# Second block's first steps: combine quarters ahead of the next transposes, and the feed-forward at a distance of seven steps

## The chip, the cores and the metric

One NeuronCore of one Trainium2 chip runs the whole program. The metric is the device time of one execution in microseconds. Every array is float32. The engines are TensorE (PE, with its weight loads PEld), VectorE (DVE), ScalarE (ACT), GpSimd (POOL) and SyncE (SP, which issues most of the DMAs).

## What is computed

The reference has two blocks over 2 sequences of 1024 tokens with 256 features. The lines that matter here, cut:

```python
# block 0: attention with a field, then a soft mixture of 64 experts
combine = softmax(logits.reshape(b, m, n * p))        # per token over 2048 slots
x = x + einsum('bnpd,bmnp->bmd', y, combine)           # "combine"
# block 1: a rotation of x, then two layers of this
x1 = rotated(x)                                        # one 256x256 matrix per token
for l in range(2):
    q, k, v = split(shift(x1) @ wqkv[l])
    q, k = rotary(l2norm(q) * qs), rotary(l2norm(k) * ks)
    x1 = x1 + local_attention(q, k, v) @ wo[l]         # windows of 128, each with the one before
    h = layernorm(shift(x1)) * lg + lb                 # over 256 features
    a, g = split(h @ w1[l] + b1[l])                    # 682 wide each
    x1 = x1 + (a * gelu(g)) @ w2[l] + b2[l]
x = x + x1
```

## The kernel before, in words

The change lies in the last part of the kernel, a loop over steps `s` whose order is written out by hand: PE, DVE, ACT and POOL execute their instructions in the order in which the loop emits them (`manual_schedule` names the four engines). SP's DMAs are not in that list; each is issued when its data and its buffer are ready.

**Attention.** There are 32 windows of 128 tokens: two layers, two sequences, eight windows. In step `s`, window `s+2` is projected (`project`, `rotate_parts`, `values`, `norms`, `rotated`), window `s+1` is transposed (`turn`), window `s` gets its scores for two groups of four heads (`scores`, `maxima`, `weights`, `divide`), and windows `s-1` and `s-2` are finished (`turn_e` transposes the weights, `mix` multiplies with the values). After each fourth window `project_out` writes 512 tokens of `xb`.

**Feed-forward.** A chunk is 512 tokens, eight chunks in all. `forward(s - LAG)` runs one quarter of a chunk at the end of a step: `gate` 0 to 5 (the gated first matrix in six pieces, the last a short one of 42 rows), `feed` (the second matrix) and, for the next chunk, `centre` (mean by a matmul with `ones_d`, subtraction on DVE, square on ACT) and `normalise` (variance by a matmul, square root on ACT, reciprocal and product on DVE, scale and shift on POOL).

**Combine.** Block 0's combine is not finished when the loop begins. Its products for sequence 1 run beside the first attention steps, at the points "a", "c" and "b" of a step, as a list `mixing` of pairs `(q, jj)`: quarter `q` of 256 tokens, and four of 16 expert groups `jj`. `turn_w(q, jj)` makes eight transposes of softmax rows into one two-bank PSUM tile, copies it to `xb` (DVE for odd `jj`, ACT for even), and fetches logits of later rows. `combine(q, jj)` multiplies by the experts' outputs (16 PE instructions of 256 columns). `weigh(i)` and `scale(i)` are the softmax of row block `i`: a maximum on DVE, an Exp on ACT, a reciprocal and product on DVE. `READY` says at which points they stand. `rotate(h)` makes 512 tokens of block 1's input.

`PARTS` puts quarters at the points: three in steps -2 and -1, two (at "a" and "b") in steps 0 to 4, so that at "a" of steps 0 to 4 the tile that is turned has odd `jj` and goes through DVE, and at "b" an even one through ACT.

**PSUM.** `two_banks` hands out two tiles (`ps_b`). While `mixing` is not empty, the third two-bank tile (`ps_c`) holds the combine's sum; afterwards the three go round in turn (`ring`). `project`, `scores`, `turn_w`, `turn_e`, `turn`, `rotate`, `project_out`, `gate` and `feed` all take their tile from here.

The order at point "a" of a step, before:

```python
project(s + 2); rotate_parts(s + 2); mix(s - 2, 1); scores(s, 0)
beside(s, "a")            # turn_w of the next quarter, then combine of this one
turn_e(s - 1, 0)
maxima(s, 0); weights(s, 0); values(s + 2)
```

Of the kernel before, what the change touches and what calls it, by code (L numbers as in the profile page):

```python
# [91 lines left out]
def tile_kernel(ctx: ExitStack, tc: tile.TileContext, a: dict, out: bass.AP):  # L92
# [80 lines left out]
    def wide(name):  # L173
        return ps_s.tile([P, 2, 512], F32, tag="s", name=name)

    def pair(name):
        return ps_t.tile([P, 2, 512], F32, tag="t", name=name)
# [147 lines left out]
    def mix(s):  # L325

        u, n, j0 = s // 16, s % 16 // 8, s % 8
        b, g = units[u]
        po = pair("po")[:, 0, :]
        for j in (j0, j0 + 1):  # L330
            for hh in range(4):
                at = (4 * g + hh) * VW
                nc.tensor.matmul(  # L333
                    po[32 * hh : 32 * hh + 32, :],
                    v[b][:, j, at : at + 32],
                    es[s + j - j0, hh // 2][:, hh % 2, :],
                    start=(j == j0),
                    stop=(j > j0),
                )
        for x in range(4):  # L340
            es.pop((s + x // 2, x % 2))
        if j0 == 0:
            obs[u, n] = at2.tile([P, 512], F32, tag="ob", name=f"ob{u}_{n}")
            nc.scalar.copy(obs[u, n], po)
            return
        if s >= STEPS - LEAD:
            nc.vector.tensor_tensor(obs[u, n], obs[u, n], po, ALU.add)
            return
        part = at2.tile([P, 512], F32, tag="part", name="part", bufs=1)
        nc.scalar.copy(part, po)  # L350
        nc.gpsimd.tensor_tensor(obs[u, n], obs[u, n], part, ALU.add)  # L351
# [466 lines left out]
    def row(i):  # L818
        return ebig[:, i % 4, :]
# [19 lines left out]
    def turn_w(q, jj):  # L839

        pt = wide("pe")
        for j in range(4):
            for i in range(2):
                nc.tensor.transpose(
                    pt[:, j // 2, (j % 2 * 2 + i) * P : (j % 2 * 2 + i + 1) * P],
                    row(2 * q + i)[:, (4 * jj + j) * P : (4 * jj + j + 1) * P],
                    ident,
                )
        wTs[q, jj] = xb[:, jj % 2, 1, 1 : 1 + S].rearrange("p (x n) -> p x n", x=2)
        if jj % 2:  # L850
            nc.vector.tensor_copy(wTs[q, jj], pt)
        else:
            nc.scalar.copy(wTs[q, jj], pt)  # L853
        for i in (2 * q + 4, 2 * q + 5):
            if i < T // P:
                fetch(i, jj)
# [156 lines left out]
    with tc.manual_schedule(  # L1013
# [15 lines left out]
        mixing, ring = [None], []  # L1029
# [164 lines left out]
        def divide(i, hg):  # L1194
            e, lo, den = scs.pop((i, hg))
            nc.vector.reciprocal(den, den)  # L1196
            engine = nc.vector if hg else nc.gpsimd
            for c in range(2):
                for x in range(2):
                    engine.tensor_scalar(e[:, x, c, lo:], e[:, x, c, lo:], den[:, x, c : c + 1], None, ALU.mult)  # L1200
            es[i, hg] = e
# [54 lines left out]
        def chunk(f):  # L1256

            return f // (B * 2), f // 2 % B, f % 2 * 512
# [27 lines left out]
        def gate(f, n):  # L1286

            l = chunk(f)[0]
            if n == 0:
                us[f] = fa["u"]  # L1290
            pt = two_banks("pga")
            gl = fa["gl"][:, n % 2, :]
            if n < NW1:
                for x, lo in ((0, W1G + n * P), (1, W1A + n * P)):
                    for k in range(2):
                        nc.tensor.matmul(  # L1296
                            pt[:, x, :], load["w1"][:, k, lo : lo + P], hcs[f][:, k, :], start=(k == 0), stop=(k == 1)
                        )
                pg, pa, m, g0 = pt[:, 0, :], pt[:, 1, :], P, 0
            else:  # L1300
                for k in range(2):
                    nc.tensor.matmul(
                        pt[: TG + TAIL, 0, :], load["w1"][:, k, W1T:W1N], hcs[f][:, k, :], start=(k == 0), stop=(k == 1)
                    )
                pg, pa, m, g0 = pt[TG : TG + TAIL, 0, :], pt[:TAIL, 0, :], TAIL, TG
            nc.scalar.activation(gl[:m, :], pg, AF.Gelu, bias=col(f"b1g{l}", n)[g0 : g0 + m, :])  # L1306
            nc.vector.scalar_tensor_tensor(
                us[f][:m, n, :], pa, col(f"b1a{l}", n)[:m, :], gl[:m, :], ALU.add, ALU.mult
            )
# [29 lines left out]
        def forward(at):  # L1339

            f, k = divmod(at, 4)
            if at == -2:
                centre(0)
            if at == -1:
                normalise(0)
            if not 0 <= f < CHUNKS:
                return
            if k == 0:
                gate(f, 0)
                gate(f, 1)  # L1350
            if k == 1:
                gate(f, 2)
                gate(f, 3)
                if f + 1 < CHUNKS:
                    centre(f + 1)
            if k == 2:
                gate(f, 4)
                gate(f, 5)
                if f + 1 < CHUNKS:
                    normalise(f + 1)  # L1360
            if k == 3:
                feed(f)


# [2 lines left out]
        mixing = [(q, jj) for q in range(4, 8) for jj in range(4)]  # L1367
# [12 lines left out]

        def beside(s, point):
            if point in PARTS.get(s, ""):
                if len(mixing) > 1:
                    turn_w(*mixing[1])
                q, jj = mixing[0]
                combine(q, jj)
                mixing.pop(0)
                if (q, jj) in ((4, 1), (6, 1)):
                    rotate(q // 2 - 1)
            for f, i in READY.get((s, point), ()):  # L1390
                f(i)

        LAG = 8
        fa = {}
        for s in range(-2, LAG + 4 * CHUNKS):
            now, before, nxt, new = (0 <= s + d < WINDOWS for d in (0, -1, 1, 2))

            if new:
                project(s + 2)
                rotate_parts(s + 2)  # L1400
            if 0 <= s - 2 < WINDOWS:
                mix(s - 2, 1)
            if now:
                scores(s, 0)
            beside(s, "a")
            if before:
                turn_e(s - 1, 0)
            if now:
                maxima(s, 0)
                weights(s, 0)  # L1410
            if new:
                values(s + 2)
                keep_values(s + 2)
            beside(s, "c")
            if now:
                scores(s, 1)
                maxima(s, 1)
            if before:
                mix(s - 1, 0)
            if nxt:  # L1420
                turn(s + 1)
            if now:
                weights(s, 1)
            if new:
                norms(s + 2)
            beside(s, "b")
            if 0 <= s - 2 < WINDOWS and (s - 2) % 4 == 3:
                project_out((s - 2) // 4)
            if before:
                turn_e(s - 1, 1)  # L1430
            if now:
                divide(s, 0)
            if new:
                rotated(s + 2)
            forward(s - LAG)
            if now:
                divide(s, 1)
            if s == 5:

                rotate(3)  # L1440
                f = xp.tile([P, 4 * NS], F32, tag="e", name="f")
                at = 0
                for name, k, n in (("u", NF, 512), ("w2", NF, D), ("yo", 2, 512), ("rs", 1, 512), ("sq", 2, 512), ("gl", 2, 512)):
                    fa[name] = f[:, at : at + k * n].rearrange("p (k n) -> p k n", k=k)
                    at += k * n
                fa["rs"] = fa["rs"][:, 0, :]
                fa["hc"] = xin.tile([P, 2, 2, 512], F32, tag="x1", name="hc")
                load["w2"] = fa["w2"]
                load["w1"] = xp.tile([P, NE // 4 * D], F32, tag="y1", name="w1")[:, : 2 * W1N].rearrange(
                    "p (k n) -> p k n", k=2  # L1450
                )
                weights2(0, "w1", "w2")
            if s + 2 == B * NWIN - 1:
                weights2(1, "wqkv", "tabs")
            if s == B * NWIN + 2:
                weights2(1, "wo")
            if s == LAG + 4 * (CHUNKS // 2) - 2:
                weights2(1, "w1")
            if s == LAG + 4 * (CHUNKS // 2) - 1:
                weights2(1, "w2")  # L1460
# [118 lines left out]
```

## Time and profile before

| | before |
|---|---|
| median of 3 runs (lowest to highest) | 1710.03 us (1709.95 to 1711.98) |
| the profiled execution | 1710.05 us |
| its span, first to last instruction | 1708.3 us |
| PE busy | 1659.0 us (97%) |
| DVE, ACT, POOL busy | 950.6 (56%), 830.1 (49%), 426.2 (25%) |
| step -2 starts (first `project`) | 889.89 us |
| step 5 starts | 1044.91 us |
| first `gate` | 1112.52 us |
| end of the last attention step's PE work (`project_out`) | about 1647 us |

The profiled execution lies 1.75 us above its span and 0.02 us above the median, so its rows can be set against the median without a correction. Two things help in reading what follows. A PE row's duration is partly modelled, and matmuls overlap, so the time that PE spends on a piece of work is read from one start to the next (16 combine matmuls: 3.46 us from the first start to the next piece's start). And a wait in brackets at the end of a row is the engine's idle time just before it, with the instruction that ended it.

### The profile page before, as it was taken

Reading aid. Unit: us, or ns where it says so; the run is one execution under the profiler, and the core shown is the slowest. Engines: PE = TensorE matmul, PEld = TensorE weight load, DVE = VectorE, ACT = ScalarE, POOL = GpSimd, SP = SyncE. Lnnn points to the kernel's source line nnn. Section 1 sums busy time; section 2 is a strip of 40 time slices with the busy share of each in tenths; the row PEclk is TensorE's granted clock in tenths of the full one; section 3 lists DMA queues with packets and bytes.
Section 4 is the critical chain, followed back from the end, with each engine's and each line's share of the span. In section 5 each row is a group of like instructions: output and inputs, shape, how many; then the busy total and the mean of one; then the engine's idle time right before and its main releaser. Section 6 shows DMA issues by size and latency. Waiting matters only on the chain.

```text
span 1708.3 us, 22359 instructions
## 1 busy us (share of the span) xinstructions
PE 1659.0 (97%) x8684; PEld 842.9 (49%) x8684; DVE 950.6 (56%) x1622; ACT 830.1 (49%) x1329; POOL 426.2 (25%) x716
## 2 busy tenths in 40 slices
PE   8999999999999999999999899999999999999998
PEld 4333443443433444444787566555555555555543
DVE  5767767766773322243445666756565656574522
ACT  1456556656667322243233444655555656565520
POOL 3101101111110100000102334645554544354301
PEclk9999999999999999999999999999999999999999
DMA  5100000000000534555542002000100001000001
GB/s 150 50 13 13 1 13 14 1 14 12 1 1 1 170 116 159 160 172 165 189 129 71 21 1 75 1 0 1 62 1 13 1 1 34 17 1 25 1 25 37
DMA packets 49593, 82.55 MB, mean 48 GB/s; under 512 B 4508, under 2 KB 24816, under 8 KB 49232
## 3 DMA queue, kind: packets, MB, share of 16 engines
q1 hardware_dynamic: 46944, 75.29, 14.5%
q0 software_dynamic: 1584, 5.29, 1.0%
q8 instruction: 68, 1.11, 0.3%
q10 hardware_dynamic: 960, 0.56, 0.1%
q14 instruction: 37, 0.30, 0.1%
HBM read 55.95 MB, written 20.97 MB: 45 GB/s over the span
## 4 chain that ended last, share of the span: by engine, by line
PE 86%; DVE 7%; ACT 4%; POOL 1%; issue 1%; DMA 1%; DVEq 0%; ACTq 0%; POOLq 0%
PE sc L314 9%; PE pga L1296 8%; PE po L333 7%; PE lg L754 7%; PE sl L780 6%; PE pm L282 6%; PE cmb L865 6%; PE py L1319 5%; PE pq L1061 4%; PE pwo L1250 3%; PE sc L1150 3%; PE pe L1211 3%; PE po L1230 3%; PE pv L1117 2%; ACT e L322 2%; PE pqk L252 2%
## 5 line engine op out<-in xcount | busy, mean ns | idle before, releaser
L289 DVE TENSOR_REDUCE mx<-pm 128x2 f32<-128x1024 f32 x256 | 304.5, 1220 | 87.5 <-PE pm L282 83.5
L322 ACT ACTIVATE e<-sc 128x1024 f32<-128x1024 f32 x256 | 253.8, 1023 | 91.4 <-PE pm L282 53.3
L282 PE MATMUL pm<-km,qm 32*128 32x512 f32 x1024 | 271.1, 635 | 3.3 <-DVE mx L289 2.1
L314 PE MATMUL sc<-qs,km 32*128 32x512 f32 x1024 | 254.4, 614 | 9.0 <-ACT e L322 8.1
L351 POOL TENSOR_TENSOR ob<-ob,part 128x512 f32<-128x512 f32 x43 | 54.5, 1267 | 421.4 <-ACT part L350 421.4
L314 PEld LDWEIGHTS sc<-qs,km 32*128 32x128 f32 x1024 | 85.7, 184 | 133.9 <-ACT e L322 68.0
L1200 POOL TENSOR_SCALAR e<-e,den 128x256 f32<-128x256 f32 (+1 forms) x128 | 131.0, 1036 | 58.1 <-DVE den L1196 58.1
L1296 PE MATMUL pga<-hc,w 128*128 128x512 f32 x320 | 141.1, 593 | 0.0
L1167 DVE CUSTOM_DVE_ANT_0 e<-sc,mask,zn 128x256 f32<-128x256 f32 (+1 forms) x256 | 103.5, 462 | 45.4 <-PE sc L1150 45.4
L1184 ACT ACTIVATE e<-e,nmx 128x256 f32<-128x256 f32 (+1 forms) x256 | 123.5, 486 | 3.1 <-DVE nmx L1167 2.9
L333 PE MATMUL po<-e,v 128*32 128x512 f32 x1024 | 123.8, 600 | 0.7 <-ACT e L322 0.6
L1085 POOL TENSOR_TENSOR t<-raw,tabs 128x512 f32<-128x512 f32 x64 | 80.2, 1274 | 168.2 <-ACT raw L1075 165.9
L780 PE MATMUL sl<-dsp,xb 128*128 128x512 f32 x256 | 116.7, 600 | 2.0 <-ACT dsp L769 2.0
L865 PE MATMUL cmb<-xb,y 128*128 128x256 f32 x512 | 117.6, 383 | 0.2 <-ACT xb L853 0.2
L1061 PE MATMUL pq<-wqo,xa 128*128 128x512 f32 x256 | 115.7, 595 | 0.7 <-ACT xa L892 0.7
L754 PE MATMUL lg<-phi,xa 128*128 128x512 f32 x256 | 115.9, 595 | 0.3 <-ACT xa L407 0.3
L865 PEld LDWEIGHTS cmb<-xb,y 128*128 128x128 f32 x512 | 95.8, 192 | 12.8 <-ACT xb L853 0.5
L1075 ACT COPY raw<-pq 128x1024 f32<-128x1024 f32 x32 | 32.4, 1012 | 134.7 <-PE pq L1061 134.7
L764 DVE TENSOR_TENSOR l<-lg,keep 128x512 f32<-128x512 f32 x32 | 22.1, 691 | 135.8 <-ACT keep L762 135.8
L1306 ACT ACTIVATE f<-pga,cols 128x512 f32<-128x512 f32 (+1 forms) x48 | 32.9, 686 | 125.8 <-PE pga L1296 118.4
L1296 PEld LDWEIGHTS pga<-hc,w 128*128 128x128 f32 x320 | 59.2, 190 | 67.7 <-issue 66.3
L282 PEld LDWEIGHTS pm<-km,qm 32*128 32x128 f32 x1024 | 77.2, 183 | 28.7 <-DVE mx L289 14.8
(199 smaller groups left out, 2429.2 us busy)
## 6 DMA issues: line engine op xcount, KB each, us to landing
lgd<-keep SPq DMA_DIRECT2D x64, 256.0 KB, 2.4
w<-in_ffn_W SPq DMA_DIRECT2D x16, 1024.0 KB, 7.3
ebig<-lgd SPq DMA_DIRECT2D x64, 256.0 KB, 3.3
wqo<-in_wqkv SPq DMA_DIRECT2D x2, 1536.0 KB, 8.9
w<-in_w SPq DMA_DIRECT2D x2, 1386.0 KB, 6.1
km<-hk SPq DMA_DIRECT2D x32, 64.0 KB, 2.3
qm<-hq SPq DMA_DIRECT2D x32, 64.0 KB, 2.4
phi<-in_phi SPq DMA_DIRECT2D x1, 2048.0 KB, 7.5
```

The lines of the kernel that those rows point to most:

```text
L282: nc.tensor.matmul(pm[:, x, :], qm[u % 2][r, i * P : (i + 1) * P], km[u % 3][r, n * 512 : (n + 1) * 512], start=True, stop=True,)
L289: nc.vector.tensor_reduce(mxs[hu][:, i % 4, 2 * half : 2 * half + 2, n], pm, AX.X, ALU.max)
L314: nc.tensor.matmul(sc[:, x, :], km[u % 3][r, j * P : (j + 1) * P], qs[u % 2][r, n * 512 : (n + 1) * 512], start=True, stop=True,)
L322: nc.scalar.activation(e, sc, AF.Exp, scale=1.0 / HD0**0.5)
L333: nc.tensor.matmul(po[32 * hh : 32 * hh + 32, :], v[b][:, j, at : at + 32], es[s + j - j0, hh // 2][:, hh % 2, :], start=(j == j0), stop=( ...
L754: nc.tensor.matmul(lg[:, b, :], xa[:, k, b, 1 + m * P : 1 + (m + 1) * P], phi[:, k, n * 512 : (n + 1) * 512], start=(k == 0), stop=(k == 1),)
L780: nc.tensor.matmul(accs[n][b][:, c, :], xo_tm[:, b * 8 + m, c * P : (c + 1) * P], d[:, b, :], start=(m == 0), stop=(m == 7),)
L865: nc.tensor.matmul(acs[q][:, c, :], y[b][:, 4 * jj + j, c * P : (c + 1) * P], eT[:, j // 2, j % 2 * 256 : (j % 2 + 1) * 256], start=(jj == ...
L1061: nc.tensor.matmul(pq[:, x, :], shifted(xa, k, b, w * WIN, P), load["wqkv"][:, k, x * 512 : (x + 1) * 512], start=(k == 0), stop=(k == 1),)
L1184: nc.scalar.activation(e[:, x, c, lo:], e[:, x, c, lo:], AF.Exp, bias=nmx[:, x, c : c + 1], scale=-1.0, accum_out=den[:, x, c : c + 1],)
L1200: engine.tensor_scalar(e[:, x, c, lo:], e[:, x, c, lo:], den[:, x, c : c + 1], None, ALU.mult)
L1296: nc.tensor.matmul(pt[:, x, :], load["w1"][:, k, lo : lo + P], hcs[f][:, k, :], start=(k == 0), stop=(k == 1))
```

## The change

Three things. In `beside`, the quarter's `combine` now comes first and the next quarter's `turn_w` after it. `LAG` goes from 8 to 7, so that each quarter of a feed-forward chunk runs one step earlier; with it the set-up of the feed-forward's buffers and its weight loads moves ahead of `forward` in step 5, and `rotate(3)` from the end of step 5 to before its scores. In `forward`, `centre` of the next chunk moves from after gates 2 and 3 to between gates 4 and 5, and `normalise` from after gate 5 to the front of the next quarter, ahead of `feed`. Since `LAG` shrinks by one and these move one quarter on, both keep their step relative to the attention. The diff, whole but for blank lines:

```diff
             if k == 1:
                 gate(f, 2)
                 gate(f, 3)
+            if k == 2:
+                gate(f, 4)
                 if f + 1 < CHUNKS:
                     centre(f + 1)
-            if k == 2:
-                gate(f, 4)
                 gate(f, 5)
+            if k == 3:
                 if f + 1 < CHUNKS:
                     normalise(f + 1)
-            if k == 3:
                 feed(f)
...
             if point in PARTS.get(s, ""):
-                if len(mixing) > 1:
-                    turn_w(*mixing[1])
-                q, jj = mixing[0]
+                q, jj = mixing.pop(0)
                 combine(q, jj)
-                mixing.pop(0)
+                if mixing:
+                    turn_w(*mixing[0])
                 if (q, jj) in ((4, 1), (6, 1)):
                     rotate(q // 2 - 1)
...
-        LAG = 8
+        LAG = 7
...
                 mix(s - 2, 1)
+            if s == 5:
+                rotate(3)
             if now:
                 scores(s, 0)
...
                 rotated(s + 2)
-            forward(s - LAG)
-            if now:
-                divide(s, 1)
             if s == 5:
-                rotate(3)
                 f = xp.tile([P, 4 * NS], F32, tag="e", name="f")
...
                 weights2(0, "w1", "w2")
+            forward(s - LAG)
+            if now:
+                divide(s, 1)
```

## The prediction

> **What bounds the kernel now.** First the engines' busy times, then PE's waits in the two stretches that the change touches, then the timeline of single steps.
>
> ```profile
> PE 1659.0 (97%) x8684; PEld 842.9 (49%) x8684; DVE 950.6 (56%) x1622; ACT 830.1 (49%) x1329; POOL 426.2 (25%) x716
> ```
>
> PE is the bound, and the change removes no PE work. It can only win or lose idle PE time. The waits (line waited for: us in total, times, longest), first for 880 to 1120 us, then for 1120 us to the end:
>
> ```profile
> PE pe L844 <- DVE t L1083: 5.7, 5, 1.8
> PE pe L844 <- DVE nmx L1167: 2.8, 2, 2.6
> PE pe L1211 <- POOL e L1200: 2.5, 5, 0.6
> ```
>
> ```profile
> PE sc L1150 <- DVE t L1083: 2.3, 4, 0.6
> PE pe L1211 <- DVE e L1200: 1.8, 3, 1.3
> ```
>
> L844 is `turn_w`: its PSUM tile is the one that `project` used, and it waits for DVE (L1083) to empty it, in steps 0 to 4. Step 3 in the timeline:
>
> ```profile
> 1005.54 1.13 PE L1150 MATMUL sc<-qkT 64*128 64x256 f32 x8
> ...
> 1006.30 1.21 DVE L1083 TENSOR_TENSOR t<-pq,tabs 128x1024 f32<-128x1024 f32 x1
> ...
> 1007.56 1.09 PE L844 MATMUL pe<-ident,ebig 128*128 128x128 f32 x8 [0.88 <-DVE t L1083]
> 1008.49 3.63 PE L865 MATMUL cmb<-xb,y 128*128 128x256 f32 x16
> 1008.69 1.22 DVE L851 COPY xb<-pe 128x1024 f32<-128x1024 f32 x1 [1.19 <-PE pe L844]
> 1009.83 0.47 DVE L1167 CUSTOM_DVE_ANT_0 e<-sc,mask,zn 128x256 f32<-128x256 f32 x1
> ...
> 1011.95 1.04 PE L1211 MATMUL pe<-ident,e 128*128 128x128 f32 x8
> ```
>
> See two things: the 0.88 us wait, and that today the product (3.46 us) covers the copy (L851) which frees the tile for `turn_e` (L1211). Two PSUM tiles are in play and `scores` holds the other until `maxima` (L1167), which DVE runs after the copy.
>
> [...] clock 0.93 in 930.5 to 953.5, and a combine that takes 5.0 us instead of 3.46 just after an idle 2.56 us. [...] Moving `normalise` away from the gates adds one load per chunk, on an ACT that is 49% busy: taken as free under `feed` (10.9 us of PE).
>
> **Part A: product first.** Durations from the rows: product 3.46, eight transposes 0.87, DVE copy 0.2 + 1.22 + 0.05 = 1.45 after the last transpose.
>
> *Point "a", steps 1 to 4.* The product now covers the wait for L1083. But `turn_e` follows the transposes at once and waits 1.45 for the copy. Gaps that go (issue to issue): 1.42, 0.84, 0.96, 0.96. So 0, +0.6, +0.5, +0.5.
>
> *Point "b".* `turn_w`'s ACT copy is then followed only by `turn_e` (0.87), and `project` needs its tile: 0.2 + 1.0 + 0.05 - 0.87 = +0.4 in steps 2 and 3. In step 1 `rotate` covers it, and the wait of 0.4 for `maxima` goes: -0.4. In step 2 a like wait of 0.3 goes.
>
> *Step 2's DVE chain.* Behind the copy stand `scale`, `weigh` and `maxima`, and PE waits for the last:
>
> ```profile
> 985.41 1.22 DVE L851 COPY xb<-pe 128x1024 f32<-128x1024 f32 x1 [1.19 <-PE pe L844]
> ...
> 986.74 1.29 DVE L837 TENSOR_SCALAR ebig<-ebig,den 128x2048 f32<-128x2048 f32 x1
> 987.94 2.28 DVE L828 TENSOR_REDUCE nmx<-ebig 128x1 f32<-128x2048 f32 x1
> ...
> 990.33 0.48 DVE L1167 CUSTOM_DVE_ANT_0 e<-sc,mask,zn 128x256 f32<-128x256 f32 x1
> ...
> 992.08 1.13 PE L1150 MATMUL sc<-qkT 64*128 64x256 f32 x8 [0.65 <-DVE nmx L1167]
> ```
>
> Scores end at 983.44; product and transposes put the copy at 987.98 instead of 985.41: the chain and this L1150 come 2.57 later. With -0.3 and +0.4 at "b" step 2 is +2.6 (its 0.6 at "a" lies inside). PE then idles 2.8 us in one piece[...]: +1.3.
>
> *Steps -1 and 0.* Product (5,1) has only `turn` (0.87) between its copy and itself: +0.6. Step 0 took 22.99 us (930.49 to 953.48) with 15.99 of work. Now its copy ends at 941.0, scale at 942.4, `weigh`'s maximum at 944.75, `maxima` at 945.9; `turn(1)`, ready at 941.9, waits for that. Then product, transposes, and `project(3)` at 951.1, plus 1.15 for the half clock up to 948.2: 952.3, so steps -1 and 0 together -1.2.
>
> Sum of A: -1.2 - 0.4 + 2.6 + 1.3 + 0.9 (step 3) + 0.5 (step 4) = **+3.7**. The logits' fetches on SP come 3.46 later; the last of rows 12 and 13 lands near 915, and its reader on DVE starts at 928. If that margin of 13 were gone, it would be paid in full.
>
> **Part B: LAG 7.** *Step 5*: `rotate` ahead of the scores covers `turn_e`'s POOL divide (row 1.37 instead of 0.87): -0.5. `centre(0)` directly follows `project_out` and must wait for its DVE add (0.2 + 1.22 + 0.05, less `turn_e` 0.87): +0.6. The w1 load was issued at 1043.17 and lands in about 6 us; its first user moves from 1112 to about 1097, so it stays hidden.
>
> *Steps 7 and 8.* Step 8 starts at 1097.30 and needs 7.7 of PE work to its second scores, but:
>
> ```profile
> 1101.26 3.35 DVE L1279 RECIPROCAL f<-f 128x512 f32<-128x512 f32 x1
> ...
> 1109.05 0.71 PE L1150 MATMUL sc<-qkT 64*128 64x128 f32 x8
> ```
>
> 3.95 is lost: POOL's divide has no feed-forward to hide under, `normalise`'s reciprocal holds DVE, and a slow window follows. With gates in step 7, step 8 loses nothing. `normalise(0)` moves to step 6: from its matmul to the second scores it took 13.45 (1095.58 to 1109.05), which puts step 7's at 1093.45 instead of 1091.69: +1.75. Net -2.2.
>
> *Steady steps.* The four waits of L1150 for L1083 (2.3) follow `normalise` at a step's end. With `feed`'s 10.9 behind it they go: -2.3. `centre` between gates 4 and 5 has the same add ahead of it and 3.43 of gate 4 as cover (6.87 before): free, and at worst 0.5 each for 7 chunks if DVE is late. At the layer's turn POOL multiplies the new tables up to 1238.0, and the step gets 1.7 shorter: up to 0.5 there.
>
> *Tail.* Step 31:
>
> ```profile
> 1610.19 0.30 PE L1211 MATMUL pe<-ident,e 128*128 128x128 f32 x1 [1.27 <-DVE e L1200]
> ...
> 1613.21 12.85 PE L1319 MATMUL py<-f 128*128 128x512 f32 x24 [0.84 <-DVE nmx L1167]
> ```
>
> 1.8 for the divide behind the reciprocal, 0.84, and `feed` 1.9 over its 10.9 at half clock: 4.5. After, `feed` covers the reciprocal in step 30 and gates stand in 31: about 0.5 is left. New: in step 34 `normalise(7)` has only gate 5 (1.72) over subtractions and square (0.2 + 1.28 + 0.1 + 1.06): +0.9. Net -3.1. One `feed` quarter fewer at the end changes no work.
>
> Sum of B: +0.1 - 2.2 - 2.3 - 3.1 = **-7.5**. Late next is `turn_e` at "a", for its own tile.
>
> **Sum**: +3.7 - 7.5 = -3.8; 1710.05 - 3.8 = **1706.2**, the same against the median, which is 0.02 lower. About 0.2% (3.4 us) is what a measurement of this kernel can tell from no change; the forecast sits just past that.
>
> **The cases.** (1) As worked out, 50%: 1702.5 to 1709, by slow windows more or fewer[...] and 0.5 per small cover. (2) Product first pays in full, 15%: `turn_e` gets the free tile and DVE its copy in time. Then 5.7 + 2.8 of waits and the slow window's 1.5 go: 1710.05 - 10 - 7.5 = 1692.5; with half of the DVE chain left, about 1700. For it speaks that PE waits most at L844, against it DVE's order in the rows above. (3) Slower, 10%: the new idle pieces at "a" of steps 1 to 4 and in steps 7 and 34 each halve the clock.[...] Against it: `turn_e`'s and `turn_w`'s transposes lie on both sides[...]. (4) The waits move rather than go, 25%: DVE's reciprocal and `feed`'s adds delay other tiles and B brings 3 instead of 7.5: 1710.7. Against it: `feed`'s 10.9 exceeds the reciprocal's 3.35, product 1.23 and POOL's 1.75 together.
>
> Faster by over 0.2%: 33 of case 1, all 15 of (2), 5 of (4) = 53%. Within: 17 and 18 = 35%. Slower: 10 and 2 = 12%. The range 1699 to 1712.5 leaves out half of (2) and the slower end.
>
> **What would show it.** Right: L844 without waits for L1083; instead L1211 waiting about 1.4 for L851 in four steps, and a second scores in step 2 waiting near 2.8 for L1167; no wait of L1150 for L1083 in the steady steps; no wait of L1211 for L1200 before the last feeds. Wrong: `turn_e` at "a" without a wait, or waits of L1211 for DVE that come back after each `feed`.

## The result, and the profile after

The changed kernel takes 1709.62 us (median of 14 runs, 1707.89 to 1710.87), the kernel before 1709.82 us on the same chips (14 runs). The ratio is 0.9996, with a 95% interval of 0.9988 to 1.0004. That is no change which can be told from none: between 2.1 us faster and 0.7 us slower. The forecast was 1706.2 us.

The two halves of the change are both large, and they cancel. The page of the profiled execution (1709.74 us, span 1707.9) has the same PE work:

```profile
PE 1658.3 (97%) x8684; PEld 844.7 (49%) x8684; DVE 949.1 (56%) x1622; ACT 839.7 (49%) x1335; POOL 425.8 (25%) x716
```

PE's waits after, for 880 to 1120 us and then to the end (line waited for: us in total, times, longest):

```profile
PE pe L1211 <- DVE xb L851: 4.2, 3, 1.4
PE pt L1135 <- DVE nmx L1167: 3.8, 1, 3.8
PE sc L1150 <- DVE nmx L1167: 2.5, 1, 2.5
PE sc L1150 <- DVE t L1083: 1.8, 1, 1.8
PE pe L1211 <- DVE den L836: 1.4, 1, 1.4
PE pe L1211 <- POOL e L1200: 1.1, 2, 0.6
...
```

```profile
PE po L1230 <- ACT eT L1217: 1.5, 2, 1.2
PE pvar L1276 <- ACT f L1269: 0.7, 1, 0.7
PE pwo L1250 <- ACT oT L1241: 0.7, 1, 0.7
```

All waits of L844 (8.5 us) are gone, and so are the four of L1150 for L1083 in the steady steps and those for L1200 near the end. In their place stand waits of `turn_e` (L1211) for the copy L851, and two long ones for `maxima` (L1167). The row with `den L836` is the same wait for the copy; another short DVE instruction ended last.

Step 3 in the timeline, the same place as before:

```profile
1011.34 1.14 PE L1150 MATMUL sc<-qkT 64*128 64x256 f32 x8
...
1011.61 1.20 DVE L1083 TENSOR_TENSOR t<-pq,tabs 128x1024 f32<-128x1024 f32 x1
1012.41 3.73 PE L865 MATMUL cmb<-xb,y 128*128 128x256 f32 x16
...
1015.97 1.04 PE L844 MATMUL pe<-ident,ebig 128*128 128x128 f32 x8
1017.05 1.22 DVE L851 COPY xb<-pe 128x1024 f32<-128x1024 f32 x1 [4.24 <-PE pe L844]
1018.19 0.47 DVE L1167 CUSTOM_DVE_ANT_0 e<-sc,mask,zn 128x256 f32<-128x256 f32 x1
1018.42 1.06 PE L1211 MATMUL pe<-ident,e 128*128 128x128 f32 x8 [1.41 <-DVE xb L851]
```

L1083 ends at 1012.8, long before the transposes, so the old wait is gone. DVE then idles 4.24 us until the transposes give it the copy, and PE stands for the length of that copy.

In step 2 the late copy moves a whole chain on DVE, and PE waits for its end:

```profile
989.71 1.22 DVE L851 COPY xb<-pe 128x1024 f32<-128x1024 f32 x1 [3.86 <-PE pe L844]
...
992.24 2.28 DVE L828 TENSOR_REDUCE nmx<-ebig 128x1 f32<-128x2048 f32 x1
...
994.62 0.47 DVE L1167 CUSTOM_DVE_ANT_0 e<-sc,mask,zn 128x256 f32<-128x256 f32 x1
...
996.37 1.21 PE L1150 MATMUL sc<-qkT 64*128 64x256 f32 x8 [2.51 <-DVE nmx L1167]
```

In step 0 it is the same chain with `turn` at its end:

```profile
941.16 1.22 DVE L851 COPY xb<-pe 128x1024 f32<-128x1024 f32 x1 [2.86 <-PE pe L844]
...
943.69 2.28 DVE L828 TENSOR_REDUCE nmx<-ebig 128x1 f32<-128x2048 f32 x1
...
946.08 0.34 DVE L1167 CUSTOM_DVE_ANT_0 e<-sc,mask,zn 128x128 f32<-128x128 f32 x1
...
947.29 1.97 PE L1135 MATMUL pt<-ident,t 128*128 128x128 f32 x8 [3.81 <-DVE nmx L1167]
...
949.05 5.54 PE L865 MATMUL cmb<-xb,y 128*128 128x256 f32 x16
```

Before, the longest wait in this step was 2.56 us, and one product was slow:

```profile
947.41 1.27 PE L844 MATMUL pe<-ident,ebig 128*128 128x128 f32 x8 [2.56 <-DVE nmx L1167]
948.48 5.17 PE L865 MATMUL cmb<-xb,y 128*128 128x256 f32 x16
```

After, both pieces of work behind the wait are slow: the transposes take 1.76 us to the next start instead of 0.93, the product 5.38 instead of 3.46. The table of stretches (start and end in us, length, busy time of PE, PEld, DVE, ACT, POOL, then PE's clock, the DMA share and GB/s) gives the clock for steps 0 and 2, where 1.00 is full speed:

```profile
932.34:955.30 22.96, 19.15 (x87) 13.87 (x85) 13.28 (x32) 11.63 (x25) 5.94 (x16) 0.85 0.16 47
...
979.78:1006.69 26.91, 22.56 (x125) 16.29 (x125) 17.14 (x39) 13.92 (x27) 9.63 (x18) 0.94 0.00 1
```

In step 0 the clock is 0.50 from 946.10 to 952.93, in step 2 from 997.30 to 1000.71. Before, it is 0.50 from 948.19 to 951.60 in step 0, from 1105.20 to 1108.61 in step 8 and from 1613.78 to 1617.19 in the `feed` of step 31. The forecast and the expectations call a stretch like these a slow window or a half-clock window.

Near the end the reciprocal now lies inside `feed`:

```profile
1606.99 11.05 PE L1319 MATMUL py<-f 128*128 128x512 f32 x24
1610.69 3.35 DVE L1279 RECIPROCAL f<-f 128x512 f32<-128x512 f32 x1 [3.90 <-ACT f L1278]
1614.08 1.22 DVE L1280 TENSOR_TENSOR hc<-hc,f 128x1024 f32<-128x1024 f32 x1
```

Lengths of the steps, from one `project` to the next, in the two profiled executions (us):

| | before | after | difference | forecast |
|---|---|---|---|---|
| step -1 | 19.02 | 19.72 | +0.70 | +0.6 |
| step 0 | 22.99 | 22.96 | -0.03 | -1.8 |
| step 1 | 24.68 | 24.48 | -0.20 | -0.4 |
| step 2 | 22.83 | 26.91 | +4.08 | +3.9 |
| step 3 | 21.87 | 23.05 | +1.18 | +0.9 |
| step 4 | 22.05 | 22.85 | +0.80 | +0.5 |
| steps -1 to 4 | 133.44 | 139.97 | **+6.53** | +3.7 |
| step 5 to the end | 663.39 | 655.31 | **-8.08** | -7.5 |

(Step 0's forecast is the -1.2 for steps -1 and 0 less the +0.6 of step -1.) The rest of the difference of the spans, +1.15, lies ahead of step -2, where nothing was changed; this point, the start of step -2, stood anywhere from 889.4 to 891.9 in the ten profiles of this case.

### The profile page after: what moved, and what is told of

It reads as the page before. It is cut to its first block, busy times and chain, and to the rows that moved or that the text cites. A ratio compares the mean times of both kernels' runs of the same rounds, so it can differ in the third digit from the quotient of the medians.

```text
span 1707.9 us, 22367 instructions
## 1 busy us (share of the span) xinstructions
PE 1658.3 (97%) x8684; PEld 844.7 (49%) x8684; DVE 949.1 (56%) x1622; ACT 839.7 (49%) x1335; POOL 425.8 (25%) x716
## 4 chain that ended last, share of the span: by engine, by line
PE 91%; DVE 3%; ACT 3%; DMA 1%; issue 1%; POOL 0%; DVEq 0%; ACTq 0%; POOLq 0%
PE sc L314 9%; PE pga L1296 8%; PE po L333 7%; PE cmb L865 6%; PE pq L1061 6%; PE pm L282 6%; PE lg L754 6%; PE sl L780 6%; PE py L1319 5%; PE po L1230 4%; PE sc L1150 4%; PE pwo L1250 3%; PE pe L1211 3%; PE pv L1117 3%; ACT e L322 2%; PE pt L1135 2%
## 5 line engine op out<-in xcount | busy, mean ns | idle before, releaser
L1200 POOL TENSOR_SCALAR e<-e,den 128x256 f32<-128x256 f32 (+1 forms) x128 | 131.0, 1036 | 57.2 <-DVE den L1196 57.2
L1167 DVE CUSTOM_DVE_ANT_0 e<-sc,mask,zn 128x256 f32<-128x256 f32 (+1 forms) x256 | 103.9, 462 | 52.1 <-PE sc L1150 52.1
L780 PE MATMUL sl<-dsp,xb 128*128 128x512 f32 x256 | 116.7, 600 | 2.2 <-ACT dsp L769 2.2
L1319 PE MATMUL py<-f 128*128 128x512 f32 x192 | 88.4, 605 | 0.0
```

Source lines behind the costliest of these rows:

```text
L780: nc.tensor.matmul(accs[n][b][:, c, :], xo_tm[:, b * 8 + m, c * P : (c + 1) * P], d[:, b, :], start=(m == 0), stop=(m == 7),)
L1319: nc.tensor.matmul(py[:, c, :], load["w2"][:m, n, c * P : (c + 1) * P], u[:m, n, :], start=(n == 0), stop=(n == NF - 1),)
```

## The experiments

The theory after the result: **two halves cancel**. Product first costs 6 to 7 us, through the copy that DVE gets too late; the feed-forward part saves about 8. The rivals: neither part moves the time by itself; or the parts depend on each other, and the feed-forward part alone brings 3 us or less. A ratio below is against the kernel before, in runs on the same chip.

### Product first alone

The kernel before, with only this edit:

```diff
-                if len(mixing) > 1:
-                    turn_w(*mixing[1])
-                q, jj = mixing[0]
-                combine(q, jj)
-                mixing.pop(0)
+                q, jj = mixing.pop(0)
+                combine(q, jj)
+                if mixing:
+                    turn_w(*mixing[0])
```

> Only the order in `beside` is changed; LAG 8 and `forward` stay as before. Theory (two halves cancel): the product-first order costs 6 to 7 us: 0.6 in step -1, about 0 in step 0 (the waits that go are eaten by two half-clock windows), 4 in step 2, 1 in steps 3 and 4 each; 1716 us. Rival (nothing moves by itself, the changed kernel equals the one before because both parts are hidden): within 1.5 us of before. Rival of the waits at L844 (8.5 us shown, so product first saves them): 1700 to 1703.

Measured: 1716.88 us, ratio 1.0045 (1.0032 to 1.0059), 7.7 us slower. The profile has the waits of the changed kernel at the same places, 3.8 and 2.5 for L1167 among them, and steps -1 to 4 take 140.17 us, as in the changed kernel (139.97). So the loss needs nothing of the other half, and the idea that L844's 8.5 us could be saved falls: they were exchanged for longer waits.

### The feed-forward part alone

The changed kernel with the edit above undone.

> The changed kernel with the old order in `beside` (transposes, then product); LAG 7 and the new `forward` stay. Theory (two halves cancel): 7.5 to 8.5 us faster than before, about 1702: steps 7 and 8 lose 2.9 instead of 5.1, the four waits of 0.57 for L1083 are gone, step 31 loses nothing to the reciprocal, step 34 pays 0.7 new. Rival (nothing moves by itself): within 1.5 us of before. Rival[...]: 3 us or less.

Measured: 1702.31 us, ratio 0.9961 (0.9949 to 0.9974), 6.7 us faster. The two parts by themselves add up to +1.0 us, the whole change to -0.7 (from its ratio): within the intervals they are additive, so the rival of a dependence is not needed. The profiles say the same with less noise. Steps -1 to 4 take 133.46 us here and 133.44 before; from step 5 to the end it is 655.36 us here and 655.31 in the changed kernel.

### The new order inside `forward`, LAG 8 kept

The kernel before, with only the hunk in `forward` from the diff of the change.

> The kernel before with only the new order inside `forward` (centre between gates 4 and 5, normalise ahead of feed), LAG 8 kept, so both come one step later against the attention. If the gain of the feed-forward half comes from normalise standing ahead of feed (reciprocal covered): the four waits of 0.57 go, and in step 31 the divide, the tile and the slow window (4.5) go, new 0.7 to 0.9 at the last normalise: 5 to 6 us faster, and steps 7 and 8 keep their loss of 5.1. If the gain comes from LAG 7 itself (gates one step earlier, a shorter tail): 2 us or less faster.

Measured: 1703.35 us, ratio 0.9967 (0.9955 to 0.9980), 5.6 us faster. So most of the second half is the new order, not the shorter distance. (This run moves `centre` together with `normalise`; that the gain is the reciprocal's, which now lies under `feed`, is read from the waits that go.) LAG 7 adds about 1 us to it, which the intervals do not separate from nothing. The profile keeps the five waits for L1200 around steps 7 and 8 (2.5 us) and has none of the steady waits for L1083.

### The late copy on ACT

The changed kernel, with the copy of the tiles that are turned at point "a" on ACT:

```diff
-        if jj % 2:
+        if jj % 2 and not (q > 5 or (q, jj) == (5, 3)):
             nc.vector.tensor_copy(wTs[q, jj], pt)
```

> The changed kernel, with the copy of the tiles that are turned at point a of steps 0 to 4 moved from DVE to ACT; nothing else. If the loss comes through DVE's order (the late copy stands ahead of scale, weigh and maxima): the wait of 3.8 in step 0 falls to about 1, the wait of 2.5 in step 2 goes, with them the three half-clock windows of these steps (4.2 us of loss), while turn_e still waits about 1.2 for its tile in four steps: 10 us faster than the changed kernel, about 1699. If the loss is only the tile (turn_e behind its own copy): 1 us faster, 1708 to 1709, and the waits for L1167 stay.

Measured: 1694.73 us, ratio 0.9913 (0.9899 to 0.9926): 14.9 us faster than the kernel before and, by the two ratios, about 14 faster than the changed one, where 10 were expected. The waits of 3.8 and 2.5 are 0.8 and nothing, and the mean clock of the profiled execution is 0.997, where the changed kernel has 0.995. The part not expected: `turn_e` waits for a copy only once. Step 3 of this kernel:

```profile
1001.07 3.73 PE L865 MATMUL cmb<-xb,y 128*128 128x256 f32 x16
...
1001.39 0.47 DVE L1167 CUSTOM_DVE_ANT_0 e<-sc,mask,zn 128x256 f32<-128x256 f32 x1
...
1004.63 1.04 PE L844 MATMUL pe<-ident,ebig 128*128 128x128 f32 x8
1005.51 1.04 PE L1211 MATMUL pe<-ident,e 128*128 128x128 f32 x8
1005.71 1.01 ACT L853 COPY xb<-pe 128x1024 f32<-128x1024 f32 x1 [3.99 <-PE pe L844]
```

`turn_e` starts before the copy has read its tile, so it does not use that tile. The other one in play is that of the scores, which `maxima` left at 1003.1. With the copy out of DVE's queue, `maxima` runs under the product.

### Old order, copy on ACT

The kernel with the feed-forward part alone, and the edit of the copy just shown.

> LAG 7 and the new `forward`, old order in `beside` (transposes first), and the point-a copies on ACT. If product first is worth something once DVE is free: the five waits of L844 for L1083 (5.7) stay, of step 0 the 0.35, 1.2 of the 2.56 and the slow window go, of step 2 the 0.65: about 1698.5, 4 us slower than product first with the copy on ACT (1694.7). If the copy's engine was all: 1694 to 1695.5.

Measured: 1698.33 us, ratio 0.9930 (0.9918 to 0.9941). With the copy on DVE, product first costs (ratio 0.9961 against 0.9996); with it on ACT, product first saves about 3 us (0.9913 against 0.9930; their intervals overlap a little, 0.9918 to 0.9926). The profiles support it: steps -1 to 4 take 129.00 us here and 125.01 with product first. The five waits of L844 for L1083 (5.7 us) are there again, as expected.

### Step 2's softmax later

The changed kernel; only `scale(14)` and `weigh(15)` move.

```diff
-            (2, "a"): ((scale, 14), (weigh, 15)),
+            (2, "m"): ((scale, 14), (weigh, 15)),
...
                 maxima(s, 0)
                 weights(s, 0)
+                beside(s, "m")
```

> The changed kernel, with scale(14) and weigh(15) of step 2 moved from point a to after the maxima and weights of the first heads; nothing else. If step 2's loss of 4 us is the DVE chain between the late copy and the maxima: the wait of 2.5 and the slow window (1.4) go, 3.5 to 4 us faster than the changed kernel, 1705.7; turn_e's wait of 1.4 stays. If it is the tile alone: within 0.5 us of the changed kernel.

Measured: 1705.81 us over 10 runs, ratio 0.9975 (0.9966 to 0.9985). Against the changed kernel's 0.9996 that is about 3.6 us, as expected. Its waits:

```profile
PE pe L1211 <- DVE xb L851: 5.6, 4, 1.4
PE pt L1135 <- DVE nmx L1167: 3.8, 1, 3.8
```

The wait of 2.5 is gone, while the four tile waits and step 0's 3.8 stay. Step 2 takes 23.66 us here, 26.91 in the changed kernel and 22.83 before, so the chain was 3.25 of the 4.08 us that it lost. What is left holds the wait for the tile (1.41) and two that are new or longer: 0.34 for `maxima` at the second `turn_e`, and 0.70 instead of 0.23 at the next `project`.

### Transposes behind `maxima`

The changed kernel, copy on DVE, but at "a" only the product, and the transposes after `values`. Everywhere else, steps -2 and -1 and point "b", the old order stands, except at "b" of step 0. The edit in the loop, without the one in `beside`:

```diff
                 keep_values(s + 2)
+            if 0 <= s and "a" in PARTS.get(s, ""):
+                turn_w(*mixing[0])
             beside(s, "c")
```

> The changed kernel, but in steps 0 to 4 only the product stands at point a, and the transposes of the next quarter come after `values`, behind `maxima`; copy on DVE as in the changed kernel. Point b as before the change except in step 0 (product first). If the loss is DVE's order (copy ahead of scale, weigh and maxima), it goes without any move to ACT: no wait of turn_e for the copy, none of the second scores in step 2, about 1.2 left in step 0: 1692 to 1694. If the copy on DVE costs wherever it stands: 1697 or more.

Measured: 1695.76 us, ratio 0.9914 (0.9901 to 0.9926), between the two expectations, 1.8 us above the first. Three waits of L844 for `maxima` (2.0 us in all) and one of 1.4 in step 0 are left. So the copy does not cost wherever it stands on DVE: behind `maxima` most of the loss goes. How much the order alone brings is not shown, because this run also has the old order at other points. The mixture below has that too, with the copies on ACT, and is about 3 us faster (0.9897).

### The mixture

Copies on ACT; product first at "a" of steps 0 to 4 and at "b" of step 0, transposes first everywhere else.

```diff
+                if 0 <= s and point == "a" or (s, point) == (0, "b"):
+                    q, jj = mixing.pop(0)
+                    combine(q, jj)
+                    turn_w(*mixing[0])
+                else:
+                    if len(mixing) > 1:
+                        turn_w(*mixing[1])
+                    q, jj = mixing[0]
+                    combine(q, jj)
+                    mixing.pop(0)
```

> As the kernel with the point-a copies on ACT, but transposes first in steps -2 and -1 and at point b of steps 1 to 4, where product first has its 0.44 (product behind its own copy) and two waits of 0.23 for the ACT copy (two issue gaps of 0.4). Theory: 0.9 to 1.2 faster than 1694.7, that is 1693.7. Rival: the old order at b brings back the waits for maxima (0.2 to 0.4): no difference.

Measured: 1692.12 us, ratio 0.9897 (0.9884 to 0.9909): the fastest here, 17.6 us ahead of the kernel before. The step over the kernel with all products first, 0.9913, is in the direction expected. By the ratios it is 2.7 us where 0.9 to 1.2 were expected, but the intervals overlap; by the profiles steps -1 to 4 take 123.74 us instead of 125.01, which is 1.3 less. Steps 0, 2 and 3 in the table of stretches:

```profile
932.46:949.60 17.14, 16.39 (x85) 11.70 (x84) 11.14 (x27) 9.44 (x22) 2.53 (x3) 1.00 0.12 33
...
973.07:995.08 22.01, 20.82 (x125) 15.14 (x125) 16.77 (x37) 14.77 (x28) 9.67 (x18) 1.00 0.00 1
995.08:1016.04 20.96, 20.96 (x135) 15.49 (x133) 11.06 (x30) 10.79 (x24) 9.56 (x18) 1.00 0.01 2
```

Step 0 takes 17.1 us instead of 23.0, at full clock, and in step 3 PE is never idle.

## Why the prediction was right or wrong

The measured time lies inside the range, and the reading that the two parts pull against each other held. The forecast of 3.8 us was too much; the measured gain is 0.7 with an interval that ends at 2.1. A gain of over 0.2%, called the likeliest outcome at 53%, did not come. In the steps of the profiles, part A cost 2.8 us more than forecast and part B saved 0.6 more.

- **Part A, point "a"**: right. `turn_e` waits for its own copy, 1.41 in the row, 1.58 from the end of the transposes' issue. I had 1.45, with 0.05 us from the end of the copy to the next matmul where the rows of step 3 have 0.15 (1018.27 to 1018.42); and the product behind the scores takes 3.56 instead of 3.46 from start to start. Steps 3 and 4 together lost 0.6 more than forecast by this.
- **Point "b"**: right in place; project waits 0.23 for the ACT copy in steps 2 and 3, 0.40 from start to start without the work of `turn_e`, as forecast.
- **Step 2's chain**: right, +4.08 against +3.9. The 1.3 in it for half clock was my estimate; the trace has 3.41 us at 0.50, from 997.30 to 1000.71. The run with the softmax moved shows that 3.25 of it is the chain.
- **Steps -1 and 0**: here is the term that failed, "1.15 for the half clock up to 948.2". It was my estimate, of 2.3 us of work at half clock. The wait of `turn(1)` was forecast at 4.0 and came at 3.81, up to 947.29. The clock was 0.50 for 6.83 us, from 946.10 to 952.93, which cost 0.83 on the transposes and 1.92 on the product, 2.75 in all. This is 1.6 of the 1.8 us that step 0 missed. In the run with the softmax moved, beside the same 3.81 us of wait (943.03 to 946.84), the half clock lasted 3.42 us, from 946.93 to 950.35; step 0 took 21.88 us instead of 22.96, though nothing ahead of this point differs between the two kernels. Two stretches of each, first the changed kernel, then that run:

```profile
946.10:949.52 3.42, 2.23 (x10) 2.13 (x11) 2.30 (x11) 3.33 (x9) 0.00 (x0) 0.50 0.00 0
949.52:952.93 3.41, 3.41 (x10) 2.66 (x9) 2.85 (x12) 3.23 (x12) 0.34 (x2) 0.50 0.00 0
```

```profile
946.93:950.35 3.42, 3.42 (x13) 3.04 (x14) 2.45 (x9) 3.42 (x12) 0.00 (x0) 0.50 0.00 0
950.35:953.76 3.41, 3.41 (x21) 3.05 (x20) 2.23 (x7) 1.95 (x9) 1.29 (x6) 1.00 0.00 0
```

So step 0 differs by 1.1 us between these two profiles. Why the half clock lasted 6.8 us in one and 3.4 in the other is not shown.

- **Part B, step 5**: `centre(0)` waits 0.53 for the add, 0.70 from start to start, near the 0.6 of the forecast. Of the 0.5 that `rotate` should have saved at `turn_e`, 0.28 came, and `rotate` itself takes 0.19 more in its new place (3.63 us instead of 3.44). The forecast had set the length of a row, 1.37, against a time from start to start, 0.87; from start to start the row took 1.21. Step 5 lost 0.7 beyond its added work instead of 0.1.
- **Steps 7 and 8**: right; the wait of 1.76 in step 7 was forecast as 1.75, and the clock is 1.00 in steps 7 and 8 (1091.80 to 1140). Steps 6 to 8 together saved 2.0 of the 2.2. (The 3.95 of the forecast is 4.05 by its own rows, 11.75 less 7.7.)
- **Steady steps and tail**: the four waits went, and of step 31's 4.5 only 0.37 is left; step 34 pays 0.75 for the 0.9 forecast. From step 9 on the profile has 6.7 us less than before (the 6.9 of gates that moved ahead taken out) where I had 5.4. The waits and the `feed` at half clock (12.85 us before, 11.05 after) account for about 5.6 of it; where the rest went is not shown. The load per chunk that the forecast took as free is a table load on ACT: 64 of 1.28 us each instead of 58.

Of the rivals, product first paying in full is refuted by the run with it alone. The slower case needed half clock after each wait of about 1.45. The clock stayed at 1.00 after the four of 1.41; it was 0.50 at the two long ones, 3.81 and 2.51. That the waits move rather than go was true of part A, and I had counted it there; for B it was not. The case as worked out ended at 1709, and the measured 1709.62 lies just above it. The whole range held because it was drawn wider than that case, up to 1712.5, so that it took in the failed term by its width.

What stays open: how much of LAG 7 beyond the new order is real, about 1 us here, which rule hands `turn_e` one tile or the other, and what makes the half clock last 6.8 us instead of 3.4.

## What to carry to other kernels

A wait that an engine shows is not a saving until you have followed the queue of the engine that ended it: here PE's product covered the wait but held back a copy that stood at the head of DVE's queue, and everything behind that copy came late. Before two pieces of work are swapped, list what the second one releases and on which queue, and try to give that release to an engine which is idle there (ACT here) or to place it behind the work that others need first. And test the parts of a change one by one: this one looked like nothing, held about 7 us of gain, and gave 17 with the copy on ACT and the order set point by point.

## What the runs showed of the hardware that was not expected

The half clock lasted 6.8 us in one profile and 3.4 in another for one and the same wait. Beside 3.81 us of idle PE in step 0 the clock was 0.50 for 6.83 us in the changed kernel (2.75 us lost), and for 3.42 us in the run with the softmax moved.

Half clock also followed a wait of about 2 us, ahead of `sl` (L780): 2.05 us in the kernel before, then 0.50 from 780.93 to 784.35, and 2.21 us in the changed kernel, then 0.50 from 782.26 to 785.68. After the four waits of 1.41 us in steps 1 to 4 of the changed kernel, with transposes on both sides, the clock stayed at 1.00.
